# A graph kernel's first pass: the edge-norm chain and the layer's messages spread over one hundred tiles, VectorE in the order of the text, and layer 0's weights in seven wide instructions

## The chip, the cores and the metric

One core of a Trainium2 chip. The metric is the device time of one launch in microseconds (us). The kernel before was run three times: median 3583.28 us, from 3580.69 to 3591.91. Engines are called by the profile's names: PE (matrix), DVE (vector), ACT (scalar), POOL (GpSimd), SP (the queue that issues plain DMAs).

## The reference

A graph of 6,250 nodes with 128 features and 100,000 edges, sorted by destination, each with one of 8 types. First come three layers of a relational convolution; then a layer norm, three rounds of degree-scaled propagation in 64 features, and a second layer norm. One layer of the first part is:

```
weight = einsum('rb,bio->rio', comp_l, bases_l)        # 8 matrices 128x128 out of 4 bases
h      = einsum('ni,rio->nro', x, weight)              # the "messages" of a node, one per type
msg    = h[src, etype]
norm   = 1 / max(cnt[dst * 8 + etype], 1)              # edges with the same destination and type
agg    = segment_sum(msg * norm, dst)
x      = agg + x @ root_l + bias_l                     # then batch norm and relu, but for the last layer
```

`norm` and the indices are the same in all three layers, so they are made once, in layer 0.

## The kernel before, in words

Edges come in tiles of 128. In every layer two passes run over them.

**The first pass** (`first_sums`) takes tiles 92 to 191, whose destinations are the first 400 nodes. For each tile POOL issues one indirect DMA that gathers 128 rows of `x` (L1064, into `gt`, 27 buffers). PE multiplies the tile by a matrix `o` that DVE has made from each edge's place and its `norm_h` (L1056 and L1058, one pair for 8 tiles); this is L1067, into the bank `ps`. DVE adds the result to `z` (L1095, "a join"). There are two banks of `ps`, each for 8 tiles, so a tile cannot start until the joins two banks back are done.

**The second pass** (`window_sums`) takes tiles 192 to 781, 590 gathers per layer. It gathers rows of `h_d`, the table of messages in DRAM, by `gidx`, and so it cannot start before all messages are stored. `gt`, L1064 and L1067 are shared with the first pass; the joins are L1655.

**What runs beside the first pass.** `of_nodes` is a generator with 62 steps: 49 blocks of messages, each of two matmuls of 512 columns (L972), two copies on ACT (L973, into `hs`, three buffers) and one 512 KB store on SP (L974); then 13 steps of `x @ root` (L985). PE's single instruction of this kind is called a half-message here: 98 in a layer. In layer 0 a second generator, `others`, makes the tables of all 100,000 edges: `gidx`, `lo` and, in `shares`, the long chain that counts equal (destination, type) pairs by scans over 98 rows of 1024 edges (L821 to L918, with `norm` last), and then `checks` (L998 to L1023). A shorter form of the same chain (104 rows of 256) runs before anything else, for the tiles of the first pass (`norm_h`). `weights` (L681, L683) makes `w0` with 32 instructions of 128x128.

**What sets the order.** The program is written down by a scheduler, which may move an instruction ahead of others on its engine when their operands allow it. An instruction that goes through `pin` is tied to the one pinned before it on its engine. Pinned before the change are `o`, the tile matmuls and the joins. The chain of `shares` and the messages are not, so their place is the scheduler's. On the chip every engine runs its list in order.

Memory matters at one place: when `others` is done, the pools `rows` and `rows2` are released, and their room is taken by later tables. POOL writes three of these (`iota_c`, `iota_s`, `iota_q`, L1137 to L1142), and so waits at that point until the chain and the checks are done. After it comes work that is spread over the second pass (`hot_counts`, `degrees`, `counts`: L1162 on); it is started by the second pass, but the scheduler may pull its first instructions forward.

Of the kernel before, what the change touches and what calls it, by code (L numbers as in the profile page):

```python
# [8 lines left out]
F32 = mybir.dt.float32  # L9
# [4 lines left out]
OP = mybir.AluOpType  # L14
# [3 lines left out]
P = 128  # L18
# [501 lines left out]
def sorted_path(  # L520
# [45 lines left out]
    W = 1024  # L566
# [190 lines left out]

    def rsqrt(pool, o, v, shape, name):

        a = pool.tile(shape, F32, name=f"{name}_a")  # L760
        b = pool.tile(shape, F32, name=f"{name}_b")
        nc.scalar.activation(a, v, AF.Sqrt)
        nc.vector.reciprocal(a, a)
        nc.vector.tensor_mul(b, a, a)
        nc.vector.tensor_mul(b, b, v)
        nc.vector.tensor_scalar(b, b, -0.5, 1.5, op0=OP.mult, op1=OP.add)
        nc.vector.tensor_mul(o, a, b)
# [46 lines left out]
    def shares(x_, q, w, dst_x_, typ, to, j, meanwhile):  # L814
# [6 lines left out]
        nc.vector.tensor_tensor(same, dst_x_[:, : w + 1], dst_x_[:, 1:], op=OP.is_equal)  # L821
        nc.vector.tensor_scalar(at_first, at, at[:, 0:1], None, op0=OP.is_equal)
        yield
        nc.vector.tensor_scalar(at_last, at, at[:, w - 1 : w], None, op0=OP.is_equal)
        nc.vector.tensor_scalar(pair, typ, 2.0, None, op0=OP.is_ge)
        yield
        for k in range(2, KP):
            nc.vector.scalar_tensor_tensor(pair, typ, 2.0 * k, pair, op0=OP.is_ge, op1=OP.add)
        yield
        nc.vector.scalar_tensor_tensor(odd, pair, -2.0, typ, op0=OP.mult, op1=OP.add)  # L830
        nc.vector.tensor_scalar(unit, odd, 4095.0, 1.0, op0=OP.mult, op1=OP.add)
        yield
        ms = [m0, m1, m2, m3]
        for k, m in enumerate(ms):
            nc.vector.memset(m[:, w:], 0.0)
            nc.vector.scalar_tensor_tensor(m[:, :w], pair, float(k), unit, op0=OP.is_equal, op1=OP.mult)
            if k % 2:
                yield
        edge_cnt = [sp.tile([q, KP], F32, name=f"edge_cnt{x_}{k}") for k in range(2)]
        through = [sp.tile([q, KP], F32, name=f"through{x_}{k}") for k in range(2)]  # L840
        for i, mask in ((0, at_last), (1, at_first)):
            for k in range(KP):
                u = sp2.tile([P, W], F32, name="u")[:q, :w]
                nc.vector.scalar_tensor_tensor(u, ms[k][:, :w], 1.0, mask, op0=OP.mult, op1=OP.mult,
                                               accum_out=edge_cnt[i][:, k : k + 1])
                if k % 2:
                    yield
            nc.vector.tensor_tensor(through[i], at_last[:, 0:1].to_broadcast([q, KP]),
                                    same[:, i * w : i * w + 1].to_broadcast([q, KP]), op=OP.mult)
# [8 lines left out]
        for k in range(2):  # L858
            pq = pqs[k]
            flow = sp.tile([KP, 2 * P], F32, name=f"flow{x_}{k}")  # L860
            nc.vector.tensor_copy(flow.rearrange("p (k q) -> p k q", k=2)[:, :, :q],
                                  pq.rearrange("p (k q) -> p k q", k=2)[:, :, :q])
            run = sp.tile([KP, q + 2], F32, name=f"run{x_}{k}")
            nc.vector.memset(run, 0.0)
            add, keep, to_ = flow[:, :q], flow[:, P : P + q], run[:, 1 : q + 1]
            if k:
                add, keep, to_ = add[:, ::-1], keep[:, ::-1], to_[:, ::-1]
            nc.vector.tensor_tensor_scan(to_, keep, add, 0.0, op0=OP.mult, op1=OP.add)
            if k == 0 and w == W:

                full = sp.tile([KP, q], F32, name="full")
                nc.vector.scalar_tensor_tensor(full[:, : q - 1], keep[:, : q - 1], 1.0, keep[:, 1:],
                                               op0=OP.mult, op1=OP.mult, accum_out=flags[:KP, 3:4])
            runs.append(run)
# [6 lines left out]
        for k in range(2):  # L881
            b = sp.tile([q, KP], F32, name=f"before_row{x_}{k}")
            nc.vector.tensor_copy(b, pbs[k])
            before_row.append(b)
        meanwhile(2)
        for k in range(KP):
            f = sp2.tile([P, W], F32, name="u")[:q, :w]
            b = sp2.tile([P, W], F32, name="u")[:q, :w]
            nc.vector.tensor_tensor_scan(f, same[:, :w], ms[k][:, :w], before_row[0][:, k : k + 1], op0=OP.mult,
                                         op1=OP.add)  # L890
            yield
            nc.vector.tensor_tensor_scan(b[:, ::-1], ms[k][:, w:0:-1], same[:, w:0:-1],
                                         before_row[1][:, k : k + 1], op0=OP.add, op1=OP.mult)
            yield
            nc.vector.tensor_tensor(f, f, b, op=OP.add)
            if k == 0:
                nc.vector.scalar_tensor_tensor(total, pair, float(k), f, op0=OP.is_equal, op1=OP.mult)
            else:
                nc.vector.scalar_tensor_tensor(f, pair, float(k), f, op0=OP.is_equal, op1=OP.mult)
                nc.vector.tensor_tensor(total, total, f, op=OP.add)  # L900
            yield
        hi_i = ms[0][:, :w].bitcast(I32)
        hi, low = ms[1][:, :w], ms[2][:, :w]
        nc.vector.tensor_copy(hi_i, total)
        nc.vector.tensor_scalar(hi_i, hi_i, 12, None, op0=OP.logical_shift_right)
        nc.vector.tensor_copy(hi, hi_i)
        yield
        nc.vector.scalar_tensor_tensor(low, hi, -4096.0, total, op0=OP.mult, op1=OP.add)
        nc.vector.tensor_sub(hi, hi, low)
        yield  # L910
        nc.vector.tensor_mul(hi, hi, odd)
        nc.vector.tensor_add(total, low, hi)
        nc.vector.tensor_scalar_max(total, total, 1.0)
# [4 lines left out]
        nc.vector.reciprocal(to, to)  # L918
# [76 lines left out]
    def checks():  # L995

        skip = wide_tiles["at_last"][:Q, :W]
        nc.vector.scalar_tensor_tensor(skip, dst_f[:, :W], 0.0, dst_f[:, 1 : W + 1], op0=OP.add,  # L998
                                       op1=OP.is_gt, accum_out=flags[:Q, 0:1])
        nc.vector.tensor_tensor(flags[:Q, 4:5], dst_f[:, W : W + 1], dst_f[:, W + 1 :], op=OP.is_gt)  # L1000
        ends = d_in.rearrange("p (h c) -> p h c", h=GPR)
        wide = sp.tile([Q, GPR], F32, name="wide")
        nc.vector.tensor_tensor(wide, ends[:, :, GE - 1], ends[:, :, 0], op=OP.subtract)
        nc.vector.tensor_scalar(wide, wide, float(WIN), None, op0=OP.is_ge)

        part = LASTW // GE * GE
        for g in range(0, LASTW, GE):
            nc.vector.tensor_tensor(flags[96:Q, 8 + g // GE : 9 + g // GE],
                                    d_in[96:, min(g + GE, LASTW) - 1 : min(g + GE, LASTW)],
                                    d_in[96:, g : g + 1], op=OP.subtract)  # L1010
        nc.vector.tensor_scalar(flags[96:Q, 8 : 9 + part // GE], flags[96:Q, 8 : 9 + part // GE], float(WIN), None,
                                op0=OP.is_ge)
        rows_but_last = sp.tile([Q, 1], F32, name="rows_but_last")
        nc.vector.tensor_scalar(rows_but_last, iota_p[:Q, :], float(Q - 1), None, op0=OP.is_lt)
        nc.vector.tensor_scalar(wide, wide, rows_but_last, None, op0=OP.mult, op1=OP.add,
                                accum_out=flags[:Q, 1:2])
        tiles_of = d_in[:HQ, :].rearrange("p (j c) -> p j c", c=P)
        span = sp.tile([HQ, J], F32, name="span")
        nc.vector.tensor_tensor(span, tiles_of[:, :, P - 1], tiles_of[:, :, 0], op=OP.subtract)
        nc.vector.tensor_scalar(span, span, float(HW), None, op0=OP.is_ge, op1=OP.add,  # L1020
                                accum_out=flags[:HQ, 5:6])
        far = sp.tile([HQ, J], F32, name="far")
        nc.vector.tensor_scalar(far, tiles_of[:, :, 0], float(HD - HW), None, op0=OP.is_gt, op1=OP.add,  # L1023
                                accum_out=flags[:HQ, 6:7])
# [4 lines left out]
    w0 = weights(0, bases_0)  # L1029

    def others():
        nc.vector.tensor_copy(src_f, src_i)
        nc.vector.tensor_copy(dst_f, dst_i)
        nc.vector.tensor_copy(typ_f, typ_i)
        yield
        nc.vector.scalar_tensor_tensor(key_f, src_f, float(R), typ_f, op0=OP.mult, op1=OP.add)
# [4 lines left out]
        for h in range(0, W, GE):  # L1041
            nc.vector.tensor_scalar(lrow[:, h : h + GE], d_in[:, h : h + GE], d_in[:, h : h + 1], None,
                                    op0=OP.subtract)
# [74 lines left out]
    def beside_layer_0(k):  # L1118
        for _ in range(1 if k >= 4 else 0):
            next(other_tiles, None)  # L1120

    first_sums(0, layer_0, NBLK + NC, HN, beside_layer_0)
# [827 lines left out]
```

## Time and profile before

| | us |
|---|---|
| median of 3 runs | 3583.28 |
| the profiled execution's own time | 3580.38 |
| its span on the core | 3578.5 |
| busy: PE / DVE / POOL / ACT | 2714.5 / 2272.8 / 2114.9 / 324.2 |
| first gather of `x` | 10.02 |
| first half-message on PE | 57.48 |
| first gather of `h_d` in layer 0 | 199.66 |
| last gather of `h_d` in layer 0 | 1022.10 |

A row of the timeline has the start, the duration, engine, line, operation, output and inputs, how many instructions were merged into it, and in square brackets how long the engine had been idle before and what ended that idle time. A float32 matmul shows as two records, so "x4" of L972 is two half-messages and "x2" of L1067 is one tile. A row of the windows has the busy time and the number of instructions of each engine in a stretch of time, then the granted PE clock, the busy share of the DMA engines and what they moved.

### The profile page before, as it was taken

The numbers are of one execution on the slowest core, as the hardware profiler recorded it, in microseconds if no ns is written. First come the engines' busy times: TensorE is split into PE (matmuls) and PEld (weight loads), VectorE is DVE, ScalarE is ACT, GpSimd is POOL, SyncE is SP. The second block draws the span as 40 slices with busy tenths as digits, with TensorE's granted clock in tenths as the row PEclk, the third lists the DMA queues.
The fourth block names the chain that finished last, engine by engine and source line by source line (L and its number), as shares of the span: only waits on it lengthen the run. The fifth ranks groups of instructions, "written<-read, shape, count | busy, mean of one in ns | idle before, by whom it ended". The sixth has DMA issues, their size and how long they took to land.

```text
span 3578.5 us, 53292 instructions
## 1 busy us (share of the span) xinstructions
PE 2714.5 (76%) x17110; PEld 2167.3 (61%) x17110; DVE 2272.8 (64%) x6623; ACT 324.2 (9%) x600; POOL 2114.9 (59%) x2083
## 2 busy tenths in 40 slices
PE   5976667677659766666765986666677679999998
PEld 3464455655545555555544565555555569999997
DVE  7678896953752766666456357666653566656566
ACT  3500000001025000000100520000001020000000
POOL 6577777677757777777776667777777710000000
PEclk9955556558569555555765985555567579999999
DMA  6611122123238222222322852222233234545442
GB/s 194 230 52 50 52 61 70 45 66 97 59 115 313 64 66 68 68 71 73 100 69 58 297 184 78 76 77 78 76 86 79 68 97 135 158 131 157 133 139 80
DMA packets 422807, 373.23 MB, mean 104 GB/s; under 512 B 89934, under 2 KB 370286, under 8 KB 422516
## 3 DMA queue, kind: packets, MB, share of 16 engines
q1 hardware_dynamic: 347832, 230.32, 21.0%
q0 software_dynamic: 66240, 135.79, 13.5%
q10 hardware_dynamic: 8444, 3.61, 0.4%
q8 instruction: 136, 2.23, 0.3%
q14 instruction: 155, 1.27, 0.1%
HBM read 250.74 MB, written 178.62 MB: 120 GB/s over the span
## 4 chain that ended last, share of the span: by engine, by line
PE 39%; DMA 37%; DVE 11%; issue 7%; POOL 5%; DVEq 0%; POOLq 0%; ACT 0%; ACTq 0%
DMA gt<-h_d,gidx 37%; PE pw L1865 15%; PE pw L972 7%; PE ps L1067 6%; POOL gt L1064 5%; PE pw L1368 3%; PE pw L1601 2%; DVE row L1587 2%; DVE had L1560 1%; PE pw L1395 1%; PE pw L985 1%; DVE dst_hot L1583 1%; DVE agg L1655 1%; PE ps L1823 1%; PE pd L1368 1%
## 5 line engine op out<-in xcount | busy, mean ns | idle before, releaser
L1064 POOL DMA_INDIRECT gt<-h_d,gidx x1770 | 1797.9, 1016 | 554.1 <-DMA gt<-h_d,gidx 221.8
L1067 PE MATMUL ps<-o,gt 128*128 128x48 f32 (+1 forms) x4140 | 1148.3, 391 | 666.8 <-DMA gt<-h_d,gidx 590.9
L1067 PEld LDWEIGHTS ps<-o,gt 128*128 128x128 f32 x4140 | 947.5, 290 | 954.2 <-DMA gt<-h_d,gidx 779.2
L1587 DVE TENSOR_SCALAR row<-iota_c,e_tab,e_tab 128x252 bf16<-128x252 int16 x1232 | 421.6, 350 | 326.2 <-PE pw L1601 324.3
L1865 PE MATMUL pw<-three,u 128*128 128x193 bf16 x7203 | 615.8, 248 | 14.2 <-issue 9.9
L1865 PEld LDWEIGHTS <-u 128*128 128x128 fp8e3 x7203 | 602.4, 98 | 21.8 <-issue 10.0
L1601 PE MATMUL pw<-dst_hot,row 128*126 128x128 bf16 x2464 | 411.9, 318 | 56.8 <-DVE row L1587 51.9
L1601 PEld LDWEIGHTS <-row 128*126 128x126 bf16 x2464 | 337.1, 225 | 74.3 <-DVE row L1587 64.1
L1560 DVE SCALAR_TENSOR_TENSOR had<-had,keep,pw 126x256 int32<-126x256 int32 x616 | 292.1, 474 | 1.9 <-PE pw L1601 1.8
L972 PE MATMUL pw<-w,xT 128*128 128x512 f32 x588 | 288.8, 622 | 0.0
L1064 POOL DMA_INDIRECT gt<-x_d,xidx x200 | 195.0, 975 | 133.7 <-DMA xc<-in_x_dram 31.9
L1655 DVE TENSOR_TENSOR agg<-agg,ps 128x48 f32 x885 | 178.6, 202 | 141.6 <-PE ps L1067 107.3
L1859 DVE TENSOR_SCALAR u<-packed 128x640 int32<-128x640 int32 (+1 forms) x243 | 127.0, 522 | 201.9 <-PE pw L1865 200.1
L1583 DVE TENSOR_TENSOR dst_hot<-iota_f,e_tab 128x512 bf16<-128x512 f32 x308 | 211.5, 687 | 0.0
L1095 DVE TENSOR_TENSOR z<-z,ps 128x56 f32 x300 | 63.0, 210 | 194.2 <-PE ps L1067 182.3
L973 ACT COPY hs<-pw 128x512 f32<-128x512 f32 x294 | 171.7, 585 | 141.3 <-PE pw L972 134.4
L1368 PE MATMUL pw<-x,u 128*128 128x385 bf16 x735 | 178.3, 385 | 6.6 <-DVE had L1560 3.3
L1064 POOL DMA_INDIRECT gt<-in_x_dram,xidx x100 | 119.3, 1193 | 77.3 <-PE ps L1067 46.3
L972 PEld LDWEIGHTS pw<-w,xT 128*128 128x128 f32 x588 | 106.1, 197 | 86.9 <-issue 80.7
L1419 DVE TENSOR_TENSOR lo_hot<-iota_f,e_tab 128x512 bf16<-128x512 f32 x196 | 134.3, 685 | 32.4 <-PE pd L1431 31.3
L1368 PEld LDWEIGHTS <-u 128*128 128x128 fp8e3 x882 | 101.3, 119 | 79.7 <-issue 40.5
L1056 DVE TENSOR_TENSOR o<-iota_f,lo 128x384 f32<-128x384 f32 x222 | 122.7, 553 | 41.0 <-PE ps L1067 41.0
(396 smaller groups left out, 1890.8 us busy)
## 6 DMA issues: line engine op xcount, KB each, us to landing
a_d<-had SPq DMA_DIRECT2D x616, 126.0 KB
h_d<-hs SPq DMA_DIRECT2D x147, 512.0 KB
packed<-a_d SPq DMA_DIRECT2D x135, 320.0 KB
packed<-a_d SPq DMA_DIRECT2D x108, 384.0 KB
gt<-h_d,gidx POOLq DMA_INDIRECT x1770, 2.5
c_d<-had SPq DMA_DIRECT2D x62, 196.0 KB
packed<-c_d SPq DMA_DIRECT2D x21, 448.0 KB
x_d<-xc SPq DMA_DIRECT2D x24, 256.0 KB
```

What stands on the lines that cost most here:

```text
L972: nc.tensor.matmul(ph, xT[:, b * P : (b + 1) * P], w[:, c : c + 512], start=True, stop=True)
L973: nc.scalar.copy(hs[:, c : c + 512], ph)
L1064: nc.gpsimd.indirect_dma_start(out=gt, out_offset=None, in_=table[:, :], in_offset=bass.IndirectOffsetOnAxis(ap=at[:, t : t + 1], axis=0))
L1067: pin(nc.tensor.matmul(pa, gt, o, start=first_, stop=last))
L1368: nc.tensor.matmul(sums[d][:, :C3D], us[d % 2][:, i, :, d // 2], x3[:, i, :], start=(c == 0 and i == 0), stop=(c * CH + i == NBLK - 1))
L1419: pin(nc.vector.tensor_tensor(hot[:, :n, :], iota_f[:, None, :].to_broadcast([P, n, P]), src_lo[:, t0 : t0 + n, None].to_broadcast([P, n, P]),
L1560: pin(nc.vector.scalar_tensor_tensor(now[:HB, : 2 * P], had[:HB, : 2 * P], keep[:HB, s : s + 1], p[:HB, : 2 * P], op0=OP.mult, op1=OP.add))
L1583: pin(nc.vector.tensor_tensor(hots[i // TS], iota_f[:, None, :].to_broadcast([P, TS, P]), flat(e_lo)[:, i : i + TS, None].to_broadcast([P, ...
L1587: pin(nc.vector.tensor_scalar(rows[i][:, : 2 * HB], iota_c[:, : 2 * HB], e_col[:, s, j : j + 1], e_val[:, s, j : j + 1], op0=OP.is_equal, ...
L1601: pin(nc.tensor.matmul(sums[s][:HB, c * P : (c + 1) * P], row[:, c * HB : (c + 1) * HB], hots[u // TS][:, u % TS, :], start=(j == 0 and c ...
L1655: pin(nc.vector.tensor_add(to, to, pa))
L1865: nc.tensor.matmul(out_of(f), bytes_[f % 2][:, d, :, f // 2], cur[:, b, :], start=(b == 0 and f % 2 == 0), stop=(c0 == NSL - 1 and d == m ...
```

## The change

Three things are changed, all in the part of layer 0's first pass.

1. Every VectorE instruction of `shares` (both times that it runs), of `checks`, of `others` and of the new weights goes through `in_order`, a wrapper that calls `pin`. DVE so runs them, `o` and the joins in the order in which the text writes them.
2. The messages and the root products of layer 0 are spread over 92 tiles (`HT - T1 - 8`) where they were spread over 66 (`HN`); a step of `others` is taken at tiles 5, 7, 10, 12, 15 and so on (33 steps, until tile 85) where one was taken at every tile from the fourth on.
3. `w0` is made by four multiplications and three additions of 128x1024 with broadcast operands, where 32 instructions of 128x128 made it. The weights of layers 1 and 2 are made as before.

```diff
+    class Pinned:
+        def __getattr__(self, name):
+            return lambda *args, **kw: pin(getattr(nc.vector, name)(*args, **kw))
+
+    in_order = Pinned()
...
-        nc.vector.tensor_tensor(same, dst_x_[:, : w + 1], dst_x_[:, 1:], op=OP.is_equal)
-        nc.vector.tensor_scalar(at_first, at, at[:, 0:1], None, op0=OP.is_equal)
+        in_order.tensor_tensor(same, dst_x_[:, : w + 1], dst_x_[:, 1:], op=OP.is_equal)
+        in_order.tensor_scalar(at_first, at, at[:, 0:1], None, op0=OP.is_equal)
...
-    w0 = weights(0, bases_0)
+
+    w0 = wp.tile([P, R * D], F32, name="w")
+    w0_r = w0.rearrange("p (r d) -> p r d", r=R)
+    comp_0 = comp_b[:, : R * NB].rearrange("p (r b) -> p r b", b=NB)
+    for b in range(NB):
+        to = w0_r if b == 0 else sp2.tile([P, W], F32, name="u").rearrange("p (r d) -> p r d", r=R)
+        in_order.tensor_tensor(to, bases_0[:, b, None, :].to_broadcast([P, R, D]),
+                               comp_0[:, :, b, None].to_broadcast([P, R, D]), op=OP.mult)
+        if b:
+            in_order.tensor_tensor(w0_r, w0_r, to, op=OP.add)
...
     def beside_layer_0(k):
-        for _ in range(1 if k >= 4 else 0):
+        if k >= 4 and k % 5 in (0, 2):
             next(other_tiles, None)
 
-    first_sums(0, layer_0, NBLK + NC, HN, beside_layer_0)
+    first_sums(0, layer_0, NBLK + NC, HT - T1 - 8, beside_layer_0)
```

Where "..." stands, the same replacement of `nc.vector` by `in_order` is made in every DVE instruction of `shares`, `checks` and `others`.

How this moves the instructions, read from the two programs as built: in PE's list the 49 transposes of `x` now all come before the first tile (16 tiles were among them). Tiles and half-messages then alternate as follows, with T for tiles counted from 0 and M for half-messages: 12 M and 12 T, 4 M, 18 M with T 12 to 15, T 16 to 23, 18 M, T 24 to 39, 4 M, T 40 to 47, 27 M, T 48 to 55, 15 M, six root products, T 56 to 79, and the other seven root products among T 80 to 87. POOL gathers all 100 tiles of the first pass and then 15 of the second before its three iotas, where the iotas came after the 67th gather. SP has three loads of `x` ahead of the load of layer 1's bases, and one after it, all ahead of the first store of messages. From about the sixteenth tile of the second pass on, the lists of all engines are the same but for a few neighbours.

## The prediction

> **What bounds the kernel now.** I read the groups, then the windows, then POOL's timeline. The groups say which queue is full:
>
> ```profile
> L1064 POOL DMA_INDIRECT gt<-h_d,gidx x1770 | 1797.9, 1016 | 554.1 <-DMA gt<-h_d,gidx 221.8
> ```
>
> The reader is to see that 1770 gathers take 1016 ns each and that the idle time before them, 554 us, is 0.31 us each: the issue gap that every gather has. Over 1770 gathers that is 1.33 us each. In the second pass POOL therefore hardly ever waits (one wait of 15 us at 646 is the exception in layer 0), and PE waits for gathers. When the second pass starts, and at what pace POOL then runs, sets the end of layer 0, and all that follows is moved by the same amount. POOL's timeline around the change:
>
> ```profile
> 75.97 0.95 POOL L1064 DMA_INDIRECT gt<-in_x_dram,xidx  x1 [0.30 <-issue]
> 88.69 0.94 POOL L1064 DMA_INDIRECT gt<-in_x_dram,xidx  x1 [11.77 <-PE ps L1067]
> ...
> 116.83 2.55 POOL L1064 DMA_INDIRECT gt<-in_x_dram,xidx  x1 [0.90 <-PE ps L1067]
> 127.05 0.94 POOL L1064 DMA_INDIRECT gt<-in_x_dram,xidx  x1 [7.67 <-PE ps L1067]
> ...
> 152.16 0.95 POOL L1064 DMA_INDIRECT gt<-in_x_dram,xidx  x1 [13.10 <-PE ps L1067]
> ...
> 166.82 0.94 POOL L1064 DMA_INDIRECT gt<-in_x_dram,xidx  x1 [4.96 <-PE ps L1067]
> ...
> 199.66 0.94 POOL L1064 DMA_INDIRECT gt<-h_d,gidx  x1 [0.30 <-PE ps L1067]
> ```
>
> The gather of tile k needs the buffer of tile k-27. Four waits, 37.5 us, lie in the first pass, all for tiles that stand on PE behind runs of half-messages. Without any wait, at the 1.25 us of undisturbed rows (0.94 + 0.30), 100 gathers from 10.02 end at 135; here the second pass starts at 199.66. That layer 1 does messages and gathers together without POOL waiting (15.12 busy of 20 and 17 gathers is a full queue) is in the windows:
>
> ```profile
> 1100.00:1120.00 20.00, 20.00 (x63) 10.20 (x62) 4.05 (x16) 12.04 (x21) 15.12 (x17) 1.00 0.89 323
> ```
>
> PE's and DVE's rows give the prices:
>
> ```profile
> 57.48 12.20 PE L972 MATMUL pw<-w,xT 128*128 128x512 f32 x24
> 94.89 0.32 PE L1067 MATMUL ps<-o,gt 128*128 128x56 f32 x2
> 95.05 1.94 PE L972 MATMUL pw<-w,xT 128*128 128x512 f32 x4
> ```
> ```profile
> 45.56 0.73 DVE L822 TENSOR_SCALAR at_first<-dst_f 98x1024 f32<-98x1024 f32 x1
> 93.10 2.35 DVE L889 TENSOR_TENSOR_SCAN u<-same,before_row,m 98x1024 f32<-98x1024 f32 x1
> 97.73 1.23 DVE L895 TENSOR_TENSOR u<-u 98x1024 f32<-98x1024 f32 x1
> 137.04 5.05 DVE L918 RECIPROCAL norm<-norm 128x784 f32<-128x784 f32 x1
> ```
>
> Two half-messages and a tile repeat every 1.94 us: 0.86 per half-message and 0.22 per tile. The first twelve took 12.20, 1.9 more than that[...].
>
> **The change part by part.** *Weights.* Removed: 32 instructions of 128x128, which follow each other by 0.19 (8 of them) and 0.26 us (24): 7.8 us. Added: seven of 1024 columns. Row L895 (1.23, two inputs, next one 1.14 later) is nearest: 8.0 us. By the Trainium skill, VectorE: DVE Perf Modes, section "The perf-mode tier table", a float32 tensor_scalar runs at twice and a tensor_tensor at one times the base rate. That speaks against the wide form, and rows L822 (0.73) and L895 (1.23) agree; but only 8 of the 32 were of the fast kind. If all had been, the change would add 4 us; by the rows it adds 0.2. Neither lies on the path, as the next part shows: `w` is not last.
>
> *Start of the messages.* The short chain now runs without the 22 weight instructions and two others between (22 x 0.26 + 0.6 + 0.7 = 7 us), but each step then waits for the one before, which the fillers hid (about 0.07 us in 35 steps and some small memsets, 3.5 us): `norm_h` at about 34 for 37.2. PE's transposes of `x` start at 31.7 for 34.87, and no tile stands between them, so ACT's second four loads are issued at 35.7 for 38.53. The later loads took 3 to 4.6 us from issue to use; with three such rounds the last block is turned at about 50 (between 47.6 and 54.5). DVE has a new wait here: the memset of the last `xc` stands between the fourth and fifth wide instruction and waits for the ninth block, until about 44; behind it three wide instructions and the first `o` are queued, so `w` is ready at 44.5 + 3 x 1.14 = 48. On SP the load of layer 1's bases waits for `w` too, with the message stores behind it, but the first store is due only after 51. So messages start at 50, not 57.48.
>
> *PE from 50.* In the list's order: 12 M and 12 T, 10.3 + 2.6 + 1.9 = 64.8; turning `src_f` 0.7; 4 M; turning `u` 0.7; 18 M and 4 T, 86; T 16-23, 88; 18 M, 103.5; T 24-39, 107; 4 M, T 40-47, 112; 27 M, 135.5; T 48-55, 137; 15 M, 150; six root products at 1.0, 156; T 56-71, 159.5; T 72-79, about 165.
>
> *DVE, in text order.* It stalls at `gidx` (until PE has turned `src_f`, 65.5; behind it the third `o` and the first joins, due on PE only at 86). Then, with 1.14 for a 1024-wide step, 2.3 for a scan, 1.15 for a pair of `o`, 0.13 for a join and 0.5 for each load of eight offsets, it reaches the 32nd join at 105 (it waits 4 us for T 24), the chain's four rounds at 113, the pair for T 72 at 150, the joins of T 56-63 at 161 to 165 (T 72 needs their bank), `norm` at 181 and the end of the checks at 187. PE's own times above are thus nowhere later because of DVE, except T 72 by some 5 us, for which POOL comes only at 184.
>
> *POOL.* Gathers 27 to 50 follow their tiles. Gather 51 needs T 24, 104. From there 49 gathers to the last one have their tiles in time, so POOL's own pace counts, and DVE disturbs it. Thirteen gathers from 93.55 to 119.38, under back-to-back scans, took 21.3 us, 1.64 each, 1.94 with the gap. The Trainium skill, SBUF — State Buffer, "Who interferes with whom", says why this speaks against the change: a DVE instruction with two SBUF inputs blocks a GpSimd instruction that reads SBUF, whole, until it ends. By that rule a gather under scans would cost up to 0.94 + 2.3 + 0.3 = 3.5, and 49 of them 172 us, a second pass at 276. The row says 1.94 at worst and 1.25 at best. I take 1.75 until 155 (29 gathers) and 1.45 for the other 20, where DVE waits or reads PSUM: 104 + 51 + 29 = 184. At the ends: 104 + 49 x 1.25 = 165, and 104 + 49 x 1.94 = 199.
>
> The messages are stored by about 154, so the table does not hold the second pass. The iotas (1.3 us, free before, in a wait of 13.10) now stand after 15 gathers of it, at about 205; they wait for the checks, 187. With 18 us to spare they cost 1.3, and every further us of delay would hold the 575 gathers behind them.
>
> *What is late next.* About 35 small DVE instructions and several `lo_hot` of 0.69 that ran in DVE's gaps at 145 to 199 now come when the second pass has begun; its third `o` is made at about 222. POOL needs it for gather 43 of the pass, at about 242, so it does not wait; but it runs its first 23 gathers at 1.4 under a full DVE: 184 + 32.2 + 1.3 = 217.5. Before, the 23rd was at 229.18. That is 11.7 less; the lists are equal from there. DVE is 91% busy until 600 (45.71 of 50 in 350 to 400) and catches up in the free 9%.
>
> Sum: 3578.5 - 12 = 3566.5 for the span. The profiled execution itself took 3580.38 and the median is 2.9 above it, so 3571.3.
>
> **The rivals.** *The tiles gain more.* If the spread chain disturbs POOL no more than 1.4 us per gather, the second pass starts at 104 + 49 x 1.4 = 173 and the gain is about 22: 3561. For it: joins and waits break up DVE's scans. Against: 1.94 measured under them.
>
> *The gain is given back.* The iotas or the lump of small instructions hold POOL for 8 to 12 us at 205 to 245; then the time is 3580 to 3584. For it: DVE has no gap from 165 on. Against: 18 us to spare at the iotas, 20 at gather 43.
>
> *DVE becomes the bound.* One pinned list means that a late instruction holds the `o` and the joins of every later tile. The place is T 72 to T 88, behind the end of the chain and the 5.05 of the reciprocal. If DVE's 120 us from 65 to 187 take a third longer (PE's turns arriving late at `gidx`, at the flow copies and at `norm`, each with the whole list behind it), T 88 comes at 235, the 15th gather waits until then for 205, and the second pass is 30 late where it was 15 early: about 3601. T 88 has 10 us to spare (195 for 205), so it costs from 10 us of lateness on, and from 22 on the change is a loss. Against it: DVE still waits twice for PE in my walk, 4 us each.
>
> *The messages do not start earlier* (loads landing as late as before): then all of PE's times move by 7, T 24 to 111, and the gain falls to 5: 3578.
>
> **How the numbers follow.** Within 0.3% (10.7 us) this measurement cannot tell a change from none. The forecast, gain 5 to 18 (3565 to 3578), gets 0.52, of which 0.42 beyond 10.7, since its middle lies there; a larger gain 0.15; given back or no earlier start 0.08; DVE the bound 0.25, because the list leaves DVE no way round a late turn. Faster is 0.42 + 0.15 = 0.57, slower 0.25, the same 0.10 + 0.08 = 0.18. The range leaves out a tenth at each side: below, the far half of the larger gain, 3558; above, the part of DVE's case beyond 3598 (3601 is its price at a third; smaller delays are likelier).
>
> **What would show it.** Right: first half-message near 50; the waits of POOL before gather 51 only; first gather of `h_d` near 184 and no wait at the iotas; layer 0's last gather near 1010 for 1022.10; layers 1 and 2 as long as before. Wrong: a wait of POOL for PE after gather 60; gathers above 1.9 us in the mean; DVE without idle time from 65 to 190 while PE waits for `o` or a join; a gap of POOL in front of the iotas.

## The result and the profile after

| | before | after |
|---|---|---|
| median of 12 runs, us | 3586.30 | 3573.65 |
| lowest and highest, us | 3580.69, 3591.91 | 3567.83, 3576.95 |
| the profiled execution's own time, its span | 3580.38, 3578.5 | 3575.73, 3573.9 |
| first half-message on PE | 57.48 | 50.74 |
| gather 51 (it needs tile 24) | 103.53 | 103.66 |
| first gather of `h_d` in layer 0 | 199.66 | 182.06 |
| 23rd gather of `h_d` | 229.18 | 216.04 |
| last gather of `h_d` in layer 0 | 1022.10 | 1010.34 |

The ratio of the medians is 0.9963, with a 95% interval from 0.9955 to 0.9972: 12.65 us less, where the forecast was 12.0 less and 3571.3 in all.

The groups of the changed kernel, in the page's form (the line numbers after L755 are 6 to 15 higher than before):

```profile
L1079 POOL DMA_INDIRECT gt<-h_d,gidx x1770 | 1812.7, 1024 | 551.4 <-DMA gt<-h_d,gidx 219.7
```

It is the same picture as before: 1770 gathers of about a microsecond with 0.31 us between them. Nothing was taken out of POOL's queue; it starts the second pass earlier. That is read from POOL's timeline, of which these are the rows with more than 1 us of idle time from gather 27 up to the second pass, the first row of the second pass, and the rows around the iotas:

```profile
55.74 0.94 POOL L1079 DMA_INDIRECT gt<-in_x_dram,xidx  x1 [6.61 <-PE ps L1082]
71.80 1.30 POOL L1079 DMA_INDIRECT gt<-in_x_dram,xidx  x1 [1.40 <-PE ps L1082]
86.42 1.41 POOL L1079 DMA_INDIRECT gt<-in_x_dram,xidx  x1 [9.44 <-PE ps L1082]
103.66 0.94 POOL L1079 DMA_INDIRECT gt<-in_x_dram,xidx  x1 [4.23 <-PE ps L1082]
...
182.06 0.94 POOL L1079 DMA_INDIRECT gt<-h_d,gidx  x1 [0.30 <-PE ps L1082]
...
204.11 0.48 POOL L1152 IOTA iota_c<- 128x392 int16 x1
204.52 0.67 POOL L1154 IOTA iota_s<- 128x616 f32 x1
205.13 0.17 POOL L1157 IOTA iota_q<- 128x1 f32 x1
205.44 1.03 POOL L1079 DMA_INDIRECT gt<-h_d,gidx  x1
```

Up to gather 51 nothing is won: it stands at 103.66 where it stood at 103.53. The gain lies behind it. Before, three waits followed (7.67, 13.10 and 4.96 us); now there is none, and 49 gathers take 78.4 us, 1.60 each, where they took 96.1. The 17.7 us won are less than the 25.7 us of waits, since a single gather is now longer there, 1295 ns in the mean for 1099. The iotas show no wait.

PE's timeline of the changed kernel shows why. These are the start of the messages, the runs of half-messages in front of tiles 24 and 48, and the tiles from 56 on:

```profile
50.74 4.57 PE L978 MATMUL pw<-w,xT 128*128 128x512 f32 x8
...
87.55 15.68 PE L978 MATMUL pw<-w,xT 128*128 128x512 f32 x36
103.06 1.89 PE L1082 MATMUL ps<-o,gt 128*128 128x56 f32 x16
...
112.34 23.44 PE L978 MATMUL pw<-w,xT 128*128 128x512 f32 x54
...
155.44 3.67 PE L1082 MATMUL ps<-o,gt 128*128 128x56 f32 x32
162.93 3.63 PE L1082 MATMUL ps<-o,gt 128*128 128x56 f32 x16 [3.82 <-issue]
```

PE has no idle time from 50.74 to the end of tile 71, and each tile after 24 is done before the gather that needs its buffer is due: tile 56 at 155.44, for gather 83 that POOL reaches at about 158. DVE's timeline has the new wait for the ninth block of `x`, and the longest wait for tiles:

```profile
45.51 0.48 DVE L787 MEMSET xc<- 128x512 f32 x1 [6.63 <-PE pw L959]
48.23 1.22 DVE L760 TENSOR_TENSOR w<-w,u 128x1024 f32<-128x1024 f32 x1
...
157.36 1.44 DVE L1110 TENSOR_TENSOR z<-z,ps 128x56 f32 x6 [5.16 <-PE ps L1082]
```

**Why the two profiled executions differ by less than the medians.** Their times differ by 4.65 us, the medians by 12.65. At the last gather of layer 0 the distance is 11.76 us. From there to the last gather of layer 2, the part that the change doesn't touch, the profiled execution of before took 1857.1 us and that of after 1863.9. A second profiled execution of the kernel before (e9, below) took 1862.2 for the same part. So this stretch varies by some 5 us between executions of one kernel, and the medians are the better measure.

### The profile page after: what moved, and what is told of

Read it like the earlier page. It is cut to its first block, busy times and chain, and to the rows that moved or that the text cites. A ratio compares the mean times of both kernels' runs of the same rounds, so it can differ in the third digit from the quotient of the medians.

```text
span 3573.9 us, 53265 instructions
## 1 busy us (share of the span) xinstructions
PE 2699.9 (76%) x17110; PEld 2160.9 (60%) x17110; DVE 2280.5 (64%) x6598; ACT 324.0 (9%) x600; POOL 2128.9 (60%) x2083
## 4 chain that ended last, share of the span: by engine, by line
PE 38%; DMA 35%; DVE 14%; issue 7%; POOL 5%; DVEq 0%; POOLq 0%; ACT 0%; SPq 0%; ACTq 0%
DMA gt<-h_d,gidx 34%; PE pw L1880 15%; PE pw L978 7%; PE ps L1082 5%; POOL gt L1079 5%; PE pw L1383 2%; DVE row L1602 2%; PE pw L1616 1%; DVE had L1575 1%; DVE lo_hot L1434 1%; PE pw L1410 1%; DVE agg L1670 1%; DVE dst_hot L1598 1%; PE pw L991 1%; DVE o L1071 1%
## 5 line engine op out<-in xcount | busy, mean ns | idle before, releaser
L1079 POOL DMA_INDIRECT gt<-h_d,gidx x1770 | 1812.7, 1024 | 551.4 <-DMA gt<-h_d,gidx 219.7
L1082 PE MATMUL ps<-o,gt 128*128 128x48 f32 (+1 forms) x4140 | 1133.7, 388 | 638.6 <-DMA gt<-h_d,gidx 561.5
```

The costliest lines, as they stand in the source:

```text
L1079: nc.gpsimd.indirect_dma_start(out=gt, out_offset=None, in_=table[:, :], in_offset=bass.IndirectOffsetOnAxis(ap=at[:, t : t + 1], axis=0))
L1082: pin(nc.tensor.matmul(pa, gt, o, start=first_, stop=last))
```

## The experiments

The chips were not all alike. The first eight runs fell on two chips on which the kernel before itself takes 4053 us (e1 to e4) and 4019 us (e5 to e8); the last four fell on one where it takes 3584. On the slower two, the gathers in the middle of layer 1's second pass come every 1.46 us instead of 1.30, though a single one is no longer (1025 ns in the mean of e5 for 1024). The granted PE clock, as a mean over the profiled execution, is 0.663 to 0.669 on these two and 0.685 to 0.689 on the others, 3% apart where the times are 12 to 13% apart; why the chips differ was not found. So ratios are compared, and times within a trace only between runs of the same kind of chip.

**e1: pins and wide weights, the old spread.**

```diff
-        if k >= 4 and k % 5 in (0, 2):
+        for _ in range(1 if k >= 4 else 0):
             next(other_tiles, None)
...
-    first_sums(0, layer_0, NBLK + NC, HT - T1 - 8, beside_layer_0)
+    first_sums(0, layer_0, NBLK + NC, HN, beside_layer_0)
```

> The changed kernel with its list of pinned VectorE instructions and its wide weights, but with the old spread: messages over 66 tiles, and a step of the long norm chain at every tile from the fifth on. Theory (the spread is what lets POOL's gathers flow; the pinned list alone has no way round a late turn): TensorE's turns of the chain's total stand before the last 31 half-messages and before tile 40, VectorE gets there at about 155, so tile 40 runs at about 182, gather 67 waits for it, and 33 gathers at 1.4 us put the second pass at about 225 where before has 199.66 and the change 182: about 25 us slower than before, 3605 to 3615. Rival (the pins and the earlier start of the messages bring the gain, the spread nothing): second pass at 182 to 190, 3570 to 3578.

Measured: ratio 1.0046 (1.0023 to 1.0068), 15.5 us more than before on that chip. PE's timeline of e1:

```profile
144.07 3.67 PE L1082 MATMUL ps<-o,gt 128*128 128x56 f32 x16 [10.33 <-DVE z L1110]
151.99 1.54 PE L801 MATMUL pw<-ident,total 98*128 98x98 f32 x8 [4.25 <-DVE total L760]
153.32 28.74 PE L978 MATMUL pw<-w,xT 128*128 128x512 f32 x62
181.89 1.89 PE L1082 MATMUL ps<-o,gt 128*128 128x56 f32 x16
```

PE waits 10.33 us for DVE's joins and 4.25 for the end of the chain; 31 half-messages stand behind it, and tile 40 comes at 181.89 (expected 182). POOL's gather 67 waits for it until 182.49, and the second pass starts at 229.19 (expected 225). Pins and wide weights without the spread are a loss on this chip: the rival of the prediction in which DVE becomes the bound is real, at another place, and the spread is what keeps the change clear of it.

**e2 and e8: the spread alone**, on the kernel before (no pins, narrow weights).

```diff
-        for _ in range(1 if k >= 4 else 0):
+        if k >= 4 and k % 5 in (0, 2):
             next(other_tiles, None)
...
-    first_sums(0, layer_0, NBLK + NC, HN, beside_layer_0)
+    first_sums(0, layer_0, NBLK + NC, HT - T1 - 8, beside_layer_0)
```

> The kernel before with the two numbers of the spread alone: messages over 92 tiles, steps of the chain at two tiles of five; no pins, narrow weights. Theory (what counts is where tile 24 and the later tiles stand on TensorE between the half-messages): here the scheduler puts tiles and half-messages nearly by turns, so tile 24 runs after about 40 half-messages at about 92 and gather 51 there; then 49 gathers at 1.6 put the second pass at 170 to 175, and the time at 3558 to 3568, faster than the change itself although the messages start late (57). Rival (pins needed): second pass at 195 or later, within 5 us of before.

> The kernel before with the spread alone, once more. Theory: without the late loads of x (two of 15 us on the slow chip) messages start at 57, tile 24 after 40 half-messages at about 97, second pass at 175 to 180, time 3562 to 3572, as good as the change or better. Rival (pins needed): second pass at 195 or later, 3580 or more.

Measured: ratios 0.9988 (0.9963 to 1.0013) and 0.9971 (0.9940 to 1.0001). Neither is clearly faster than before. The second pass starts at 201.22 and 201.06: the expected 170 to 180 was wrong. PE's timeline of e2:

```profile
65.67 1.09 PE L953 MATMUL pw<-ident,xc 128*128 128x128 f32 x4 [14.14 <-DMA xc<-in_x_dram]
81.81 1.09 PE L953 MATMUL pw<-ident,xc 128*128 128x128 f32 x4 [15.05 <-DMA xc<-in_x_dram]
```

The loads of `x` come late, messages start at 85 instead of 57, and POOL waits 32 us for tile 16. In e8 three such waits (7.81, 13.18 and 6.62 us) lead to the same 84. Both have the first 16 tiles between the transposes of `x`, so that gathers 27 to 42 are issued while `x` is loaded; in e1, e4, e5 and e6, where the tiles stand behind the transposes, messages start at 51 to 53 on the same chips. That the gathers delay the loads would fit this, but other runs speak against it: e3 and e7, on the same chips, have the 16 tiles between the transposes too, and their messages start at 57.06 and 57.98. The kernel before has them there as well, and starts at 57.48 on the faster chip; no trace of it on a slower chip was taken. Why the loads are late in e2 and e8 stays open. What the spread alone would bring on a chip like the first one stays open.

**e3 and e7: narrow weights, not pinned**, in the changed kernel.

```diff
-    w0 = wp.tile([P, R * D], F32, name="w")
-    w0_r = w0.rearrange("p (r d) -> p r d", r=R)
...
+    w0 = weights(0, bases_0)
```

> The changed kernel with the 32 narrow weight instructions of before, not pinned. Theory (the weights do not matter for the time): the first tiles move ahead of the messages, messages start at 50 to 58, tile 24 at 98 to 106, second pass at 176 to 185, time within 5 us of the change (3569 to 3578). Rival (the wide weights are the gain, since they free the short norm chain): norm_h ready 3 us later, everything on TensorE 7 us later, second pass at 189, 3580.

> The changed kernel with the narrow, unpinned weights, once more. On the slow chip its messages stood still between 60 and 80, where copies of x landed late. Theory (the chip, not the kernel): without that stall messages start at 57, tile 24 at 103 to 110, second pass at 182 to 190, time 3573 to 3582. Rival (x loads that share the DMA queues with gathers 27 to 42 are late on any chip, and the wide weights are worth it since they hold those gathers back): second pass at 200 or later, 3590 or more.

Measured: ratios 1.0025 (1.0003 to 1.0047) and 1.0011 (0.9975 to 1.0048); second pass at 224.51 and 221.97. Messages start at 57.06 and 57.98, and then PE stands still several times until 78 (3.28, 0.40, 1.76, 1.44 and 2.11 us in e3), while ACT's first copy of a half-message comes only at 70.41. The expected 176 to 190 was missed by over 30 us. The edit moves two things: the width, and the first 16 tiles, which the scheduler puts ahead of the messages again, as in e2. So it could not tell what the width does; e12 can.

**e5: the change again**, on the second of the slower chips.

> The changed kernel as it is, as a control for the runs beside it, since the chip of the first four runs needed 13% more time for the kernel before (4053 us for 3586). If its longer gathers and stores are a matter of the chip: second pass at 180 to 186 and a ratio near 0.9965 on a chip like the first; on a slow chip the second pass between the 201 of the spread alone and the 176 of the pinned messages, and 4010 to 4040.

Measured: 4012.57, ratio 0.9966 (0.9939 to 0.9993), as on the first chip. The second pass starts at 206.88, not between 176 and 201. PE's timeline of e5 shows what is later there:

```profile
122.54 2.07 PE L978 MATMUL pw<-w,xT 128*128 128x512 f32 x2 [4.04 <-issue]
...
132.16 5.49 PE L978 MATMUL pw<-w,xT 128*128 128x512 f32 x6
...
162.94 1.89 PE L1082 MATMUL ps<-o,gt 128*128 128x56 f32 x16
```

Runs of half-messages are broken by idle time for which the trace names no reason. From 112 to 136 PE is busy for 16.23 of 24 us, at a granted clock of 0.68, where the first chip's trace has 24.00 at 1.00; the three half-messages from 132.16 on, at a clock of 0.50, take 5.49 us, twice their price. Tile 48 comes at 162.94 where it came at 135.62 on the first chip; POOL's gather 75 waits 13.84 us for it.

**e4 and e6: the half-messages of layer 0 pinned too**, in the changed kernel.

```diff
-            nc.tensor.matmul(ph, xT[:, b * P : (b + 1) * P], w[:, c : c + 512], start=True, stop=True)
+            half = nc.tensor.matmul(ph, xT[:, b * P : (b + 1) * P], w[:, c : c + 512], start=True, stop=True)
+            if l == 0:
+                pin(half)
```

> The changed kernel with the half-messages of the first layer put into TensorE's list of pinned instructions too, so that they stand between the tiles as the text has them: tile 24 after 34 half-messages instead of 52. Theory (POOL's three waits before gather 51, 15 us, come from tiles behind runs of half-messages): tile 24 at about 88, POOL has no wait after gather 27 at about 54, 73 gathers at 1.6 us put the second pass at 170 to 172, 10 to 12 us before the change: 3560 to 3565. Rival (VectorE is by now the bound, its joins and one-hots come no earlier): POOL waits for tiles from about gather 60 on, second pass at 180 to 184, time as the change, 3570 to 3576.

> The changed kernel with the half-messages of layer 0 pinned between the tiles, once more beside the change. Theory (earlier tiles let POOL start the second pass earlier, and this is handed down to the end): the second pass 6 us before that of the change (176 for 182), and the time 5 to 7 us below it, 3567 for 3573 on a chip like the first. Rival (the 47 us gained on the slow chip come from the order of the messages itself): 30 us or more below the change on any chip.

Measured: ratios 0.9900 (0.9865 to 0.9935) and 0.9901 (0.9862 to 0.9940), 47 and 35 us less than before and, in e6, 28 us less than the change beside it. POOL's timeline of e6, with its longest waits behind gather 27 and the first gather of the second pass:

```profile
54.67 0.94 POOL L1081 DMA_INDIRECT gt<-in_x_dram,xidx  x1 [2.19 <-PE ps L1084]
65.92 1.96 POOL L1081 DMA_INDIRECT gt<-in_x_dram,xidx  x1 [1.07 <-PE ps L1084]
116.08 3.60 POOL L1081 DMA_INDIRECT gt<-in_x_dram,xidx  x1 [1.41 <-remote]
...
174.25 0.94 POOL L1081 DMA_INDIRECT gt<-h_d,gidx  x1 [0.31 <-issue]
```

Gather 51 stands at 90.63 instead of 112.63, and behind gather 27 no tile is waited for longer than 2.6 us in either run, so the theory's mechanism is there. The second pass starts at 174.25 (175.85 in e4; 176 and 170 to 172 were expected), 32.6 us before the change on this chip and 7.8 before the change on the first one. By the last gather of layer 0 it is 38.6 us ahead of e5, at the end of layer 2 40.1. The theory's 5 to 7 us were missed: the 28 us in the medians come near the 30 or more that the rival named, but not for its reason: the change alone loses 24.8 us more in its first pass here than on the first chip (206.88 for 182.06), in the runs of half-messages that e5 shows, and this kernel doesn't have such runs. On a chip like the first one it was not timed; from the starts of the second pass, 174.25 for 182.06, some 5 to 8 us over the change are left there. This is an estimate across two kinds of chip; its lower end takes off the third of a head start that other traces lose later in the layer.

**e9: the kernel before again**, for its trace beside e10 to e12.

> The kernel before as it is, for its trace on the kind of chip that the experiments get. Theory (the gain of the change is the earlier second pass, handed down): the second pass 8 to 16 us later than in the change here, at 215 to 223 for 207, behind runs of half-messages (waits of POOL of 8 us and more for tiles), and that distance still there at the last gather. Rival (here the gain arises elsewhere): second pass within 3 us of the change's 207.

This time the chip was one of the faster kind. Measured: 3581.32 in the profiled execution. POOL's timeline of e9:

```profile
88.91 0.95 POOL L1064 DMA_INDIRECT gt<-in_x_dram,xidx  x1 [10.61 <-PE ps L1067]
...
127.23 0.94 POOL L1064 DMA_INDIRECT gt<-in_x_dram,xidx  x1 [6.43 <-PE ps L1067]
153.12 0.95 POOL L1064 DMA_INDIRECT gt<-in_x_dram,xidx  x1 [13.94 <-PE ps L1067]
167.78 0.94 POOL L1064 DMA_INDIRECT gt<-in_x_dram,xidx  x1 [4.96 <-PE ps L1067]
...
200.50 0.94 POOL L1064 DMA_INDIRECT gt<-h_d,gidx  x1 [0.30 <-PE ps L1067]
```

The four waits and the start of the second pass repeat within about 1 us those of the first trace. Against the trace of the change the last gather of layer 0 is 10.9 us later, that of layer 2 9.3 later. The second pass itself starts 18.4 us later, more than the 8 to 16 that were expected for a slower chip. The distance is made in the first pass, and 10.9 of the 18.4 are left at the end of layer 0.

**e10: what the chain costs POOL.** On the kernel with pinned messages, the long chain is left out: `norm` is set to one.

```diff
-        for _ in shares("", Q, W, dst_f, typ_f, norm, J, lambda k: None):
-            yield
+        in_order.memset(norm, 1.0)
```

> The kernel with pinned messages, with the long norm chain left out: norm is set to one, so the sums of the second pass are not normalised. It shows what VectorE's chain costs POOL. Theory (gathers run at POOL's own pace, and it is VectorE's two-input instructions that stretch it from 1.25 to about 1.65 us): gathers 40 to 100, which took 100.7 us with the chain, take 60 x 1.3 = 78, the mean row about 1.0 us, second pass at 152. Rival (the pace is the DMA queues', shared with 49 stores of half a megabyte): 95 us or more, second pass at 168 or later.

Measured: 3553.05 us in two runs, ratio 0.9915 (0.9894 to 0.9936). The views that tell most are POOL's groups in the same stretch, 104 to 154 us, first of the changed kernel, then of e10 (gathers, busy time, mean ns, idle time before them):

```profile
L1079 POOL DMA_INDIRECT gt<-in_x_dram,xidx x30 | 42.4, 1412 | 13.1 <-PE ps L1082 5.4 <-PE pw L978 3.0 <-issue 2.1
```
```profile
L1080 POOL DMA_INDIRECT gt<-in_x_dram,xidx x37 | 36.3, 982 | 14.6 <-PE ps L1083 7.3 <-issue 4.6 <-PE pw L978 2.7
```

With the chain a gather occupies POOL for 1412 ns, without it for 982, in a stretch in which PE makes half-messages and SP stores them in both. In e6, which has e10's order of the messages and the chain, gathers 51 to 99 take 1.36 us in the mean, so it isn't the order. DVE's chain is what stretches the gathers, by some 0.4 us each; the stores are not. Gathers 40 to 90 come every 1.38 us, and the 60 from gather 40 on take 91.5 us, between the theory's 78 and the rival's 95. The second pass nevertheless starts at 166.78 and not at 152, because of one wait, by e10's timelines of POOL and PE:

```profile
165.54 0.94 POOL L1080 DMA_INDIRECT gt<-in_x_dram,xidx  x1 [9.42 <-PE ps L1083]
```
```profile
155.50 9.60 PE L993 MATMUL pw<-xT,root_s 128*128 128x512 f32 x22
164.94 1.89 PE L1083 MATMUL ps<-o,gt 128*128 128x56 f32 x16
```

Eleven root products stand in front of tile 72, and gather 99 waits for it. Without DVE in the way, PE's order is the bound again.

**e11: the messages held back.** Eight idle instructions behind the weights of the changed kernel.

```diff
+    for _ in range(8):
+        in_order.tensor_tensor(w0_r, w0_r, w0_r, op=OP.max)
```

> The changed kernel with eight idle wide instructions behind the weights (the larger of w and w, written to w), 9.2 us of VectorE: messages start at about 58.7 instead of 52.2 here. Theory (POOL follows TensorE up to gather 51, so the earlier start of the messages is worth its full size): tile 24 and gather 51 later by 6 to 9, second pass at 213 to 216 for 207, time 6 to 9 us above the change. Rival (POOL's own pace makes it up): second pass at 207 to 209, time as the change.

Measured: ratio 0.9985 (0.9974 to 0.9997), against 0.9963 for the change: 0.22% of 3584, 7.9 us, of its 12.65 are lost. PE's and POOL's timelines of e11:

```profile
59.62 2.90 PE L978 MATMUL pw<-w,xT 128*128 128x512 f32 x3 [8.18 <-DVE w L760]
113.70 1.89 PE L1084 MATMUL ps<-o,gt 128*128 128x56 f32 x16
```
```profile
114.30 0.94 POOL L1081 DMA_INDIRECT gt<-in_x_dram,xidx  x1 [4.63 <-PE ps L1084]
192.68 0.94 POOL L1081 DMA_INDIRECT gt<-h_d,gidx  x1 [0.30 <-PE pw L991]
```

Messages start 8.9 us later than in the change (59.62 for 50.74), gather 51 and the second pass both come 10.6 later, and the last gather of layer 0 7.0 later. The absolute times of the expectation were set for a slower chip. Of its shifts, the 6 to 9 us in the time were met (7.9); gather 51 and the second pass moved by a little more, as the messages did. POOL makes none of it up in the first pass.

**e12: narrow weights, pinned**, at the place of the wide ones.

```diff
-        in_order.tensor_tensor(to, bases_0[:, b, None, :].to_broadcast([P, R, D]),
-                               comp_0[:, :, b, None].to_broadcast([P, R, D]), op=OP.mult)
...
+            if b == 0:
+                in_order.tensor_scalar(ws, bases_0[:, b, :], c, None, op0=OP.mult)
+            else:
+                in_order.scalar_tensor_tensor(ws, bases_0[:, b, :], c, ws, op0=OP.mult, op1=OP.add)
```

> The changed kernel with the 32 narrow weight instructions at the place of the seven wide ones, pinned as they are. Theory (width does not matter, only the memset that stands between them): 27 narrow ones behind the memset take 27 x 0.26 = 7.0 us instead of 3.5, w is ready at about 53 for 49.5, and the first half-message is at 53 for 52.2: second pass 1 to 4 us later, at 208 to 211, time 1 to 4 us above the change. Rival (the wide weights are what brought the gain over the kernel before): second pass at 215 or later.

Measured: ratio 0.9970 (0.9959 to 0.9981), about 2.5 us above the change; the two intervals overlap. DVE's timeline of e12:

```profile
44.71 0.48 DVE L787 MEMSET xc<- 128x512 f32 x1 [9.05 <-PE pw L959]
...
53.14 1.12 DVE L760 SCALAR_TENSOR_TENSOR w<-bs,comp_b,w 128x128 f32<-128x128 f32 x3
```

The 27 narrow instructions behind the memset take from 45.11 to 54.26, 0.34 each where 0.26 was expected, and the second pass starts at 185.77, 3.7 us after that of the change. By the last gather of layer 0 it is 1.2 us behind the change. So the wide weights are worth 3.7 us at the start of the second pass, not through their own length but through what stands behind the memset; how much of this reaches the total is not resolved. They are not what brought the gain.

## Why the prediction was right, and where not

*The start of the messages.* `norm_h` was done at 34.26 (34), the memset ran at 45.51 (until 44), `w` was ready at 49.45 (48) and messages started at 50.74 (50). The seven wide instructions took 4.69 and 3.54 us, 8.23 in all (8.0). That the width of the weights does not matter was wrong by 3.7 us at the second pass: the step's comparison of 8.0 with 7.8 took the narrow ones as they ran in before, where others stood between them. In pinned order, where three of four need the result of the one before, e12 measures 0.34 us instead of 0.26, and only the part behind the memset counts: 3.54 us for three wide ones, 9.15 for 27 narrow ones. A side sum of this step is wrong as well: 32 narrow instructions at its 0.19 us would take 6.1 us, so the wide form would add 1.9 to that and not 4.

*PE's order.* Tile 24 at 103.06 (103.5), tile 56 at 155.44 (156), tile 72 at 162.93 (165), all from the list's order with 0.86 us for a half-message and 0.22 for a tile. The first half-messages of before cost 1.9 us above this price, at a granted clock of 0.50 from 57 to 60 and of 1.00 from 65 on. The walk took the 1.9 over, and the change's trace has the low clock too, 0.50 from 50 to 52 and 0.83 from 52 to 54. This walk gave the result: e11 moves its start and moves gather 51 with it, e4 and e6 change its order and take the waits away.

*POOL's pace.* From gather 51 to the one at 153.91 there are 29 in 50.25 us, 1.73 each (1.75); the next 20 took 28.15, 1.41 each (1.45); the second pass started at 182.06 (184). The reason given was that DVE disturbs POOL, and e10 shows it, 1412 ns against 982. The Trainium skill, SBUF — State Buffer, "Who interferes with whom", has a DVE instruction with two SBUF inputs block a GpSimd instruction that reads SBUF until it ends. From this the step made up to 3.5 us for every gather. Row by row the trace agrees with the page; these are two gathers, each followed by the DVE instruction in which it starts:

```profile
117.84 2.89 POOL L1079 DMA_INDIRECT gt<-in_x_dram,xidx  x1 [0.30 <-PE pw L978]
117.64 2.35 DVE L760 TENSOR_TENSOR_SCAN u<-m,before_row,same 98x1024 f32<-98x1024 f32 x1
...
175.82 0.94 POOL L1079 DMA_INDIRECT gt<-in_x_dram,xidx  x1 [0.30 <-issue]
175.22 5.05 DVE L760 RECIPROCAL norm<-norm 128x784 f32<-128x784 f32 x1
```

The first ends at 120.73, 0.74 after its scan; the second, beside a longer instruction with one input, takes its usual 0.94. Of the 49 gathers, 15 are longer than 1.2 us. All of them start inside a DVE instruction with two SBUF inputs, nine end 0.74 to 0.82 us after it, and six, with more DVE work close behind it, 1.09 to 1.35 after it. The other 34 take 0.95 us in the mean. So a gather loses only what is left of the instruction in which it starts, and most lose nothing. That is why the mean, with the gap, is 1.60 us and not 3.5, and why taking the measured row was right.

*The iotas and what is late next.* They took 1.33 us (204.11 to 205.44, expected 1.3 at 205), without a wait; the checks ended at 185.4 (187). The 23rd gather came at 216.04 (217.5), 13.1 us earlier than before (11.7). "The lists are equal from there", so that the distance stays, was right only roughly: by the last gather of layer 0 it was 11.76. In five traces of the faster kind with the whole chain (both of before, the change, e11, e12), the second pass of layer 0 takes the longer the earlier it starts: 828.3 us from 182.06, 825.8 from 185.77, 824.7 from 192.68, 822.4 and 820.8 from 199.66 and 200.50. A third of a head start or a little more is eaten there, in this range. Between the 200th and the 250th gather of the pass alone, the change's lead over the other four shrinks by 2.6, 3.8, 1.1 and 2.5 us (both of before, e11, e12). What eats it was not tried. That 12.0 meets 12.65 so closely is thus partly luck: the lead at the second pass was larger than forecast (17.6 us for 15.7), and the loss behind it was larger too.

*The base.* The sum started from the median of three runs, 3583.28; that of twelve was 3586.30. By the difference, 12.0 us forecast and 12.65 measured, the sum was better than by the time, 3571.3 for 3573.65.

*The rivals.* More than 22 us from the tiles would have needed 1.4 us per gather under the chain; it was 1.73. The gain was not given back at the iotas. DVE did not become the bound, since its waits for PE, 9.48, 4.02 and 5.16 us, were left; e1 shows that with the old spread it does. And the case in which the messages do not start earlier, for which 3578 was worked out, is what e11 makes: 3577.9 us, 5.6 less than before on its chip, where the gain was to fall to 5.

## What to carry to other kernels

Where two engines take turns with a ring of buffers, ask for each item at what place it stands on the engine that frees its buffer, and walk that list with the row's prices: here the gain was three waits behind runs of matmuls, and the start of the second pass could be worked out within 2 us. Pinning an engine's list was a gain here only with the work that the list serves spread over the same stretch; the same pins with the old spread cost 15 us on a slower chip. And once some of the order is written by hand, the rest can be worth writing too: pinning the messages as well brought more than the change itself on the chips where it was timed.

## What was not expected

- The kernel before took 3584 or 3586 us on some chips and 4019 and 4053 on others. The ratio of the change was the same on two kinds, 0.9963 and 0.9966; that of the pinned messages can't be carried over like that, as the change's first pass is 24.8 us longer on one than on the other.
- Narrow VectorE instructions of 128x128, three of four of which need the result of the one before, took 0.34 us from start to start; with others between them 0.26.
- A gather's time on POOL is not a constant of the gather: 982 ns in the mean beside a VectorE that is busy for 12.85 of 50 us, 1412 beside the chain of 1024-wide instructions (40.57 of 50). What counts is whether it starts inside an instruction with two SBUF inputs.
